# A cross-attention block: another order of the matmuls in the main loop, SyncE's queue ordered by hand, and another order of loads for the first two pairs

## The chip, the cores and the metric

The kernel runs on one core of a Trainium2 chip. A core has five engines that run side by side and wait for one another through semaphores: TensorE (PE, matmuls), VectorE (DVE), ScalarE (ACT), GpSimd (POOL) and SyncE (SP, which here only issues DMAs). ScalarE issues some DMAs too. The metric is the device time of one execution in microseconds, as the median of several runs. The profile shows one execution.

## What is computed

Inputs are `x` and `ctx_1024`, both 128 sequences of 128 tokens with 256 features, in float32. Every sequence goes through one block:

```python
q = (x @ Wq + bq), k = (ctx @ Wk + bk), v = (ctx @ Wv + bv)      # 16 heads of 16
scores = q k^T / sqrt(16);  scores = where(j < i, scores, -1e30)
attn = softmax(scores);  attn[:, :, 0, :] = 0
a = (attn v) @ Wo + bo
h = layer_norm(x + a, ln1_g, ln1_b)
out = layer_norm(h + relu(h @ W1 + b1) @ W2 + b2, ln2_g, ln2_b)   # W1: 256 x 1024
```

## The kernel before

**Tiles.** The 128 sequences are handled as 64 pairs `p` (256 tokens). Tokens of a pair are brought in twice: as blocks of 32 x 32 (`xb`, `cb`, `load`, line 80), which a VectorE block transpose turns into feature-major `xT` and `cT` (`tokens`, line 241), and as rows (`x`, `load_tokens`, line 97), which become the residual `xb` after `bov_r` is added (`add_bo`, line 248).

**One pair's way through the engines.** `queries`, `keys` and `values` (lines 265 to 311) are projections with full 128 x 128 matmuls; ScalarE copies their results out of PSUM into `qT`, `kT` and `vz`, and `values_out` issues a DMA that fills `vd` from ScalarE's queue. `scores(p, hi)` (line 315) makes the scores in small tiles of 32 rows x 64 columns: `hi` = 1 are queries 64 to 127 against 128 keys (16 matmuls of 256 columns), `hi` = 0 are queries 0 to 63 against 64 keys (16 matmuls of 128 columns); because of the mask the others are not needed. Softmax goes round three engines: VectorE adds the mask and takes the maximum (`mask`, `maximum`), GpSimd subtracts it, ScalarE takes the exponential (`exponential`), VectorE sums and inverts, GpSimd multiplies (`sums`). The upper scores are handled in two halves, `ONE` and `TWO`, the lower ones in one piece, `ALL`.

The weights must be transposed before they meet the values. `turn` (line 382) transposes 32 x 32 blocks on VectorE into `tb`, three instructions, and then moves the blocks between partitions by 16 DMAs `pT <- tb` on SyncE. For the first pairs and the last one `turn_on_pe` (line 406) does it on TensorE. `weigh` (line 424) multiplies `pT` with `vz` and `vd` in tiles of 128 x 32 into `pc`; `context` copies `pc` to `cxT`; `attention_out` makes `po`, `attention_sum` adds the residual and takes the statistics of the first norm, `norm1` applies it, and `turn_x1` brings the result into feature-major `x1T` by four DMAs to device memory and one back (`across`, line 230), all on SyncE.

The feed-forward part is `hidden` (`ph`, relu on ScalarE into `hT`) and `second` (`py`), 16 full matmuls each; `second_sum`, `stats`, `scale_and_shift`, `norm2`, `finish` and `store` make and store the second norm. `store` issues its DMA on ScalarE.

**The order.** `tc.manual_schedule` (line 60) says that TensorE, VectorE, ScalarE and GpSimd execute their instructions in the order in which the Python code calls them. SyncE is not in the list: a scheduler chooses the order of its DMAs. The loop at line 790 is software-pipelined. In step `p` it makes the scores and softmax of pair `p`, the context of pair `p - 1`, the projections of `p + 1`, the token transposes of `p + 2`, the hidden layer of `p - 2` and the second layer of `p - 3`. On TensorE a step of the main part reads: upper scores of `p`, `py` first half, lower scores of `p`, `py` second half, `pc`, `pq`, `po`, `pk`, `pv`, `ph`. Steps 2 to 5 have a `plan` of their own, in which the feed-forward part is filled in.

The first two pairs are written out (lines 712 to 779). `fold_norm1` computes, once, `W1`'s product with the first norm's shift (16 products of one column), `scale_w1` scales W1 by its gain, `fold_values` makes `bov_r`.

**Buffers.** `tb` and `pT` have one buffer each, `xT`, `cT`, `qT`, `kT`, `hT` two, and a bank of PSUM is one of four in turn (`bank`). Each DMA signals one of eight semaphores in turn, and a DMA waits until the one that used its semaphore before has landed, whichever queue issued it.

Of the kernel before, what the change touches and what calls it, by code (L numbers as in the profile page):

```python
# [13 lines left out]
P = 128  # L14
# [5 lines left out]
def tile_cross_attention_block(  # L20
# [26 lines left out]
    H = 16  # L47
# [9 lines left out]

    ET = mybir.EngineType
    ctx.enter_context(
        tc.manual_schedule(engines={ET.PE, ET.DVE, ET.Activation, ET.Pool})  # L60
    )

    const = ctx.enter_context(tc.tile_pool(name="const", bufs=1))
# [32 lines left out]

    def load_tokens(g, us=slice(0, 4)):
        if g not in tokens_of:
            tokens_of[g] = loads.tile([P, 4, D], F32, tag="x", name=f"x_{g}")
        nc.sync.dma_start(  # L100
            tokens_of[g][:, us], x[4 * g + us.start : 4 * g + us.stop].rearrange("b p d -> p b d")
        )


    def weight(w, name):
        n = w.shape[0] // P
        t = const.tile([P, n, w.shape[1]], F32, tag=name, name=name)
# [31 lines left out]
    table = const.tile([P, 2, 1], F32, tag="table", name="table")  # L139
    nc.scalar.activation(table, power, AF.Exp)  # L140

    b1_c = column(b1, "b1_c")
    w1 = weight(W1, "w1")
    load([1])
    wo = weight(Wo, "wo")
    bo_r = row(bo, "bo_r")
    load_tokens(0, slice(2, 4))
    g1_r = row(ln1_g, "g1_r")
    be1_r = row(ln1_b, "be1_r")
    bv_c = chunks(bv, "bv_c")  # L150
    g1_c = chunks(ln1_g, "g1_c")
    be1_c = chunks(ln1_b, "be1_c")
    load([2, 3])
    load_tokens(1)
    b2_r = row(b2, "b2_r")
    w2 = weight(W2, "w2")
    g2_r = row(ln2_g, "g2_r")
    be2_r = row(ln2_b, "be2_r")
    be1b_r = const.tile([P, D], F32, tag="be1b_r", name="be1b_r")
# [219 lines left out]

    def turn(p):


        st = states[p]
        tb = soft.tile([P, NS, (H + HH) * 32], F32, tag="tb", name=f"tb_{p}")
        at = 0
        for hi in (1, 0):
            sm = st["sm", hi].rearrange("p h j -> p (h j)")
            for t in range(sm.shape[1] // 1024):  # L390
                nc.vector.transpose(  # L391
                    tb[:, :, at : at + 256].rearrange("p j (n a) -> p n j a", a=32),
                    sm[:, t * 1024 : (t + 1) * 1024].rearrange(
                        "p (n j a) -> p n j a", j=NS, a=32
                    ),
                )
                at += 256
        pT = soft.tile([P, NS, (H + HH) * 32], F32, tag="pT", name=f"pT_{p}")
        for i in range(NS):
            for j in range(NS):  # L400
                nc.sync.dma_start(  # L401
                    pT[32 * j : 32 * j + 32, i, :], tb[32 * i : 32 * i + 32, j, :]
                )
        st["pT"] = pT.rearrange("p i (n a) -> p i n a", a=32)

    def turn_on_pe(p, hi, ts):

# [78 lines left out]
    def attention_sum(p):  # L486
        st = states[p]
        t1 = st["t1"] = ffn.tile([P, 2, D], F32, tag="t1", name=f"t1_{p}")
        nc.vector.tensor_tensor(
            t1, st.pop("po").rearrange("p (s d) -> p s d", s=2), st.pop("xb"), ALU.add  # L490
        )
        stats(p, t1, 1)
        deviation(p, 1)

    def norm1(p):
# [53 lines left out]

    b1e_c = const.tile([P, FC], F32, tag="b1e_c", name="b1e_c")  # L550

    def fold_norm1():

        ps = bank("ps_b1")
        for f in range(FC):
            for k in range(KC):
                nc.tensor.matmul(
                    ps[:, f : f + 1], w1[:, k, f * P : (f + 1) * P], be1_c[:, k : k + 1],
                    start=(k == 0), stop=(k == KC - 1),
                )  # L560
        nc.vector.tensor_tensor(b1e_c, ps[:, :FC], b1_c, ALU.add)

    def scale_w1():
        for k in range(KC):
# [33 lines left out]
        for k in range(KC):  # L598
            nc.scalar.copy(st["x1T"][:, :, :, k, :], pt[:, k])  # L599

    def hidden(p, fs):
        st = states[p]
        if fs[0] == 0:
            st["hT"] = ffn.tile([P, FC, TP], F32, tag="hT", name=f"hT_{p}")
        for f in fs[::2]:
            ph = bank(f"ph_{p}_{f}")
            for i in range(2):
                for k in range(KC):
                    nc.tensor.matmul(  # L609
                        ph[:, i * TP : (i + 1) * TP].rearrange("p (s i a) -> p s i a", s=2, a=32),  # L610
                        w1[:, k, (f + i) * P : (f + i + 1) * P], st["x1T"][:, :, :, k, :],
                        start=(k == 0), stop=(k == KC - 1),
                    )
            for i in range(2):
                nc.scalar.activation(  # L615
                    st["hT"][:, f + i, :], ph[:, i * TP : (i + 1) * TP], AF.Relu,
                    bias=b1e_c[:, f + i : f + i + 1], scale=1.0,
                )

    def second(p, s, fs=range(FC)):  # L620
        st = states[p]
# [102 lines left out]
    exponential(0, 1, ONE)  # L724
    values_out(0)
    maximum(0, 0, ALL)
    exponential(0, 1, TWO)
    queries(1)
    sums(0, 1, ONE)
    sums(0, 1, TWO)  # L730
    exponential(0, 0, ALL)
    keys(1)
    sums(0, 0, ALL)
    for which in "xc":
        tokens(2, which)
    values(1)
    values_out(1)
    fold_values()
    add_bo(0)
    load([4, 5])  # L740
    load_tokens(2)
    turn_on_pe(0, 1, range(2))
    scores(1, 1)
    mask(1, 1, 0)
    maximum(1, 1, ONE)
    turn_on_pe(0, 1, range(2, 4))
    turn_on_pe(0, 0, range(2))
    mask(1, 1, 1)
# [12 lines left out]
    queries(2)  # L761
    sums(1, 1, ONE)
    norm1(0)
# [11 lines left out]
    add_bo(1)  # L775
    add_bo(2)
    feed([("hidden", 0, 0)])
    turn_on_pe(1, 1, range(4))
# [7 lines left out]
        4: ([("hidden", 2, 0)], [("hidden", 2, 1)], [("second", 2, 0)]),  # L786
        5: ([("second", 2, 1)], [("hidden", 3, 0)], [("hidden", 3, 1)]),
    }
    waiting, late = [], []
    for p in range(2, NP):  # L790
        soon, end = p + 1 < NP, p == NP - 1
        first, then, finally_ = plan.get(
            p, ([("second", p - 3, 0)], [("second", p - 3, 1)], both("hidden", p - 2))
        )
        scores(p, 1)
        mask(p, 1, 0)
        maximum(p, 1, ONE)
        feed(first)
        mask(p, 1, 1)
        maximum(p, 1, TWO)  # L800
        scores(p, 0)
        mask(p, 0, 0)
        mask(p, 0, 1)
        exponential(p, 1, ONE)
        maximum(p, 0, ALL)
        exponential(p, 1, TWO)
        feed(then)
        sums(p, 1, ONE)
        sums(p, 1, TWO)
        summed = late + sum_up(first + then)  # L810
        exponential(p, 0, ALL)
        sums(p, 0, ALL)
        for q in waiting:
            finish(q)
        weigh(p - 1)
        context(p - 1)
        if soon:
            queries(p + 1)
        attention_out(p - 1)
        if not end:  # L820
            turn(p)
        attention_sum(p - 1)
        if soon:
# [44 lines left out]
    attention_out(p)  # L868
    second(p - 2, 1, range(FC // 2, FC))
    attention_sum(p)  # L870
    second_sum(p - 2)
    hidden(p - 1, range(FC))
    norm1(p)
# [72 lines left out]
```

## Time and profile before

| what | value |
| --- | --- |
| median of 3 runs | 1624.45 us (1621.69 to 1626.28) |
| the profiled execution | 1624.0 us, of it span 1622.2 us |
| busy TensorE / VectorE / GpSimd / ScalarE | 1602.6 / 1315.3 / 1274.9 / 765.6 us |
| granted clock of TensorE in the first three stretches of 40 us | 0.92, 0.95, 1.00 |
| DMAs `pT <- tb` | 976 on SyncE, 96 KB each, 2.1 us to landing |
| DMAs `out` and `vd` | 63 and 64 on ScalarE, 4.1 and 3.6 us to landing |
| mean busy share of the 16 DMA engines, per 40 us of the main part | about 0.6 |

Times are counted from the start of the span. A line of the timeline gives start, length, engine, line of the kernel, operation, what is written and read, the shapes, and the number of instructions merged; in brackets stands the idle time before it and what ended it. SPq and ACTq are the DMA-issuing sides of SyncE and ScalarE. A float32 matmul appears as two passes, so `pq`'s four matmuls are x8. The length of a matmul line includes the draining of the last pass, which overlaps the next line; from start to start is what it takes.

### The profile page before, as it was taken

How to read it: one execution, taken by the hardware profiler on the slowest of the kernel's cores; microseconds unless marked ns; L12 is line 12 of the kernel's file. 1: busy time of each engine (PE TensorE's matmuls, PEld its weight loads, DVE VectorE, ACT ScalarE, POOL GpSimd, SP SyncE). 2: the span in 40 equal slices, each digit the busy share in tenths (PEclk: the TensorE clock that was granted, in tenths of full speed). 3: DMA queues.
4: the chain of work that ended last, by engine and by line, in shares of the span. 5: the costliest groups of instructions: out<-in, count | busy, mean ns of one | idle time of the engine just before them, and what ended most of it. 6: DMA issues, size and time to landing. Idle time of an engine off the chain costs nothing.

```text
span 1622.2 us, 41250 instructions
## 1 busy us (share of the span) xinstructions
PE 1602.6 (99%) x16532; PEld 1338.3 (83%) x16532; DVE 1315.3 (81%) x1988; ACT 765.6 (47%) x1500; POOL 1274.9 (79%) x1105
## 2 busy tenths in 40 slices
PE   8999999999999999999999999999999999999998
PEld 6788888888888888888888888888888888888887
DVE  5789788888888888888888888888888888888852
ACT  4544444544444544444444445445444444445442
POOL 5788787887887887887887878878878878878882
PEclk9999999999999999999999999999999999999999
DMA  9345655656565665665565555566656656556430
GB/s 182 70 102 125 141 130 132 136 130 144 133 138 128 135 139 138 133 131 133 131 145 133 132 136 131 131 144 137 135 131 133 139 138 133 129 134 133 112 82 27
DMA packets 479998, 208.80 MB, mean 129 GB/s; under 512 B 352064, under 2 KB 448320, under 8 KB 479808
## 3 DMA queue, kind: packets, MB, share of 16 engines
q1 hardware_dynamic: 394864, 181.24, 50.2%
q10 hardware_dynamic: 84944, 24.92, 6.5%
q8 instruction: 132, 2.16, 0.6%
q14 instruction: 58, 0.48, 0.1%
HBM read 69.48 MB, written 32.24 MB: 63 GB/s over the span
## 4 chain that ended last, share of the span: by engine, by line
PE 94%; SPq 3%; DVE 1%; DMA 1%; issue 1%; POOL 0%; ACT 0%; POOLq 0%; ACTq 0%; DVEq 0%
PE py L625 27%; PE ph L609 26%; PE pq L259 7%; PE po L463 7%; PE pss L325 7%; PE pk L259 7%; PE pv L291 6%; PE pc L444 3%; PE pc L434 2%; SPq L401 1%; SPq L93 1%; PE py L637 1%; DVE sm L342 1%; DVE nmx L353 0%; PE ptp L417 0%
## 5 line engine op out<-in xcount | busy, mean ns | idle before, releaser
L354 POOL TENSOR_TENSOR sm<-sm,nmx 128x1024 f32<-128x1024 f32 x192 | 364.5, 1899 | 189.2 <-DVE nmx L353 185.8
L609 PE MATMUL ph<-x1T,w 128*128 128x256 f32 x2048 | 454.1, 379 | 2.1 <-ACT x1T L599 2.1
L625 PE MATMUL py<-w,hT 128*128 128x256 f32 x1952 | 453.6, 385 | 0.0
L609 PEld LDWEIGHTS ph<-x1T,w 128*128 128x128 f32 x2048 | 388.5, 190 | 56.8 <-ACT x1T L599 3.2
L625 PEld LDWEIGHTS py<-w,hT 128*128 128x128 f32 x1952 | 361.0, 190 | 76.9 <-ACT hT L615 21.9
L342 DVE TENSOR_TENSOR sm<-pss,neg 128x1024 f32<-128x1024 f32 (+1 forms) x256 | 237.7, 949 | 190.4 <-PE pss L325 190.4
L361 ACT ACTIVATE sm<-sm 128x1024 f32<-128x1024 f32 x192 | 203.0, 1058 | 342.5 <-POOL sm L354 342.4
L375 POOL TENSOR_TENSOR sm<-sm,rs 128x1024 f32<-128x1024 f32 x192 | 359.4, 1901 | 2.8 <-DVE rs L374 2.8
L615 ACT ACTIVATE hT<-ph,b1e_c 128x256 f32<-128x256 f32 x512 | 214.4, 471 | 184.7 <-PE ph L609 149.9
L391 DVE STREAM_TRANSPOSE tb<-sm 128x1024 f32<-128x1024 f32 x183 | 220.4, 1230 | 33.1 <-POOL sm L375 23.8
L353 DVE TENSOR_REDUCE nmx<-sm 128x8 f32<-128x1024 f32 (+1 forms) x192 | 234.2, 1220 | 6.6
L373 DVE TENSOR_REDUCE su<-sm 128x8 f32<-128x1024 f32 (+1 forms) x192 | 229.5, 1195 | 1.1 <-ACT sm L361 0.8
L281 ACT ACTIVATE kT<-pk,bkh,half 128x256 f32<-128x256 f32 x256 | 123.8, 565 | 160.4 <-PE pk L259 160.4
L325 PE MATMUL pss<-kT,qT 32*64 32x256 f32 (+1 forms) x4096 | 127.7, 334 | 5.7 <-DVE sm L342 3.4
L259 PE MATMUL pq<-xT,wq 128*128 128x256 f32 x512 | 129.6, 397 | 0.0
L463 PE MATMUL po<-wo,cxT 128*128 128x256 f32 x512 | 122.9, 384 | 1.4 <-ACT cxT L456 1.4
L509 POOL TENSOR_TENSOR x1b<-x,g_r 128x512 f32<-128x512 f32 x64 | 81.5, 1274 | 53.6 <-DVE x L501 53.6
L291 PE MATMUL pv<-wv,cT 128*128 128x256 f32 x512 | 121.0, 379 | 0.0
L259 PE MATMUL pk<-cT,wk 128*128 128x256 f32 x512 | 121.0, 379 | 0.0
L325 PEld LDWEIGHTS pss<-kT,qT 32*64 32x64 f32 x4096 | 76.5, 131 | 53.6 <-issue 41.8
L463 PEld LDWEIGHTS po<-wo,cxT 128*128 128x128 f32 x512 | 98.2, 192 | 15.4 <-ACT cxT L456 1.6
L259 PEld LDWEIGHTS pk<-cT,wk 128*128 128x128 f32 x512 | 97.4, 190 | 13.3
(86 smaller groups left out, 1687.6 us busy)
## 6 DMA issues: line engine op xcount, KB each, us to landing
pT<-tb SPq DMA_DIRECT2D x976, 96.0 KB, 2.1
out_dram<-t ACTq DMA_DIRECT2D x63, 256.0 KB, 4.1
xb<-in_x_dram SPq DMA_DIRECT2D x124, 128.0 KB, 4.4
cb<-in_ctx_dram SPq DMA_DIRECT2D x124, 128.0 KB, 4.4
x<-in_x_dram SPq DMA_DIRECT2D x31, 512.0 KB, 4.3
x1t<-tbx SPq DMA_DIRECT2D x236, 64.0 KB, 1.8
x1T<-x1t SPq DMA_DIRECT2D x59, 256.0 KB, 3.1
vd<-vz ACTq DMA_DIRECT2D x64, 128.0 KB, 3.6
```

What stands on the lines that cost most here:

```text
L259: nc.tensor.matmul(ps[:, m * TP : (m + 1) * TP], w[:, k, m * P : (m + 1) * P], src[:, k, :], start=(k == 0), stop=(k == KC - 1),)
L291: nc.tensor.matmul(pv[:, s * D : (s + 1) * D], st["cT"][:, k, s * P : (s + 1) * P], wv[:, k, :], start=(k == 0), stop=(k == KC - 1),)
L325: nc.tensor.matmul(sps[r // 2][s * HP : (s + 1) * HP, r % 2, m * 2 * n : (m + 1) * 2 * n].rearrange("p (e j) -> p e j", e=2), st["qT"][str ...
L342: nc.vector.tensor_tensor(st["sm", hi][:, part, :].rearrange("p (r n) j -> p r n j", r=2), st["sps", hi][t][:, :, : 4 * n].rearrange("p r ...
L353: nc.vector.tensor_reduce(nmx[:, part], sm[:, part, :], AX.X, ALU.max, negate=True)
L354: nc.gpsimd.tensor_tensor(sm[:, part, :], sm[:, part, :], nmx[:, part, None].to_broadcast([P, part.stop - part.start, n]), ALU.add,)
L373: nc.vector.tensor_reduce(su, sm[:, part, :], AX.X, ALU.add)
L375: nc.gpsimd.tensor_tensor(sm[:, part, :], sm[:, part, :], rs[:, :, None].to_broadcast([P, part.stop - part.start, n]), ALU.mult,)
L391: nc.vector.transpose(tb[:, :, at : at + 256].rearrange("p j (n a) -> p n j a", a=32), sm[:, t * 1024 : (t + 1) * 1024].rearrange("p (n j ...
L463: nc.tensor.matmul(po[:, s * D : (s + 1) * D], cxT[:, k, s, :], wo[:, k, :], start=(k == 0), stop=(k == KC - 1),)
L609: nc.tensor.matmul(ph[:, i * TP : (i + 1) * TP].rearrange("p (s i a) -> p s i a", s=2, a=32), w1[:, k, (f + i) * P : (f + i + 1) * P], st[ ...
L625: nc.tensor.matmul(st["py"][:, s * D : (s + 1) * D], st["hT"][:, f, s * P : (s + 1) * P], w2[:, f, :], start=(f == 0), stop=(f == FC - 1),)
```

## The change

**SyncE by hand.** SyncE joins the list of engines that keep the order of the code. The loads for later pairs are issued at the head of a step (`load_ahead`), the row tokens together with the context blocks, and the token buffer has two parts instead of three.

**A new step for pairs 7 to 62** (`steady`). On TensorE it reads: upper scores of `p`, both halves of `py`, `pc`, lower scores of `p`, `pq`, `po`, `pk`, `pv`, `ph`. VectorE, ScalarE and GpSimd follow that order: the context transpose of `p + 2` stands behind the upper maxima, the upper weights are transposed before the lower sums, the lower ones after the statistics and the token transpose. `turn` is split into `turn` (one block transpose) and `bring` (DMAs); eight of the 16 DMAs `pT <- tb` stay on SyncE, and eight go to ScalarE's queue between the relus of `hidden`: two behind the chunk pair 2, two behind 4, four behind 6. Pairs 2 to 6 and 63 keep the old step, with all 16 on SyncE.

**The first two pairs.** The loads of W1 come later, blocks of pairs 2 and 3 earlier; the token transposes of pair 1 and 2 are spread out; `fold_norm1` moves behind the lower scores of pair 1, and its sum with `b1` becomes `add_b1` behind the maxima.

```diff
-        tc.manual_schedule(engines={ET.PE, ET.DVE, ET.Activation, ET.Pool})
+        tc.manual_schedule(engines={ET.PE, ET.DVE, ET.Activation, ET.Pool, ET.SP})
...
-            tokens_of[g] = loads.tile([P, 4, D], F32, tag="x", name=f"x_{g}")
+            tokens_of[g] = loads.tile([P, 4, D], F32, tag="x", name=f"x_{g}", bufs=2)
...
-    b1_c = column(b1, "b1_c")
-    w1 = weight(W1, "w1")
     load([1])
     wo = weight(Wo, "wo")
     bo_r = row(bo, "bo_r")
+    bv_c = chunks(bv, "bv_c")
+    b1_c = column(b1, "b1_c")
+    g1_c = chunks(ln1_g, "g1_c")
+    be1_c = chunks(ln1_b, "be1_c")
+    load([2, 3], "x")
+    w1 = weight(W1, "w1")
+    load([2, 3], "c")
     load_tokens(0, slice(2, 4))
...
-    load([2, 3])
-    load_tokens(1)
     b2_r = row(b2, "b2_r")
     w2 = weight(W2, "w2")
+    load_tokens(1)
...
+    def bring(p, queue, which):
...
+        for u in which:
+            i, j = u // NS, u % NS
+            queue.dma_start(
+                st["pT whole"][32 * j : 32 * j + 32, i, :], st["tb"][32 * i : 32 * i + 32, j, :]
+            )
...
-    for which in "xc":
-        tokens(1, which)
     mask(0, 1, 1)
     maximum(0, 1, TWO)
-    fold_norm1()
     scores(0, 0)
+    tokens(1, "x")
+    exponential(0, 1, ONE)
+    values_out(0)
+    queries(1)
+    sums(0, 1, ONE)
     mask(0, 0, 0)
     mask(0, 0, 1)
+    tokens(1, "c")
...
     maximum(1, 1, TWO)
+    tokens(2, "x")
     weigh(0)
     context(0)
     scores(1, 0)
-    scale_w1()
+    fold_norm1()
...
     attention_out(0)
     exponential(1, 1, TWO)
+    scale_w1()
+    tokens(2, "c")
+    add_b1()
     attention_sum(0)
+    attention_stats(0)
...
+    def load_ahead(p):
+        if p % 2 == 0 and p + 4 < NP:
+            load([p + 4, p + 5], "x")
+        if p % 2 == 1 and p + 3 < NP:
+            load([p + 3, p + 4], "c")
+            load_tokens((p + 3) // 2)
+
+    def steady(p):
+        nonlocal waiting, late
+        scores(p, 1)
+        mask(p, 1, 0)
+        maximum(p, 1, ONE)
+        second(p - 3, 0)
+        mask(p, 1, 1)
+        maximum(p, 1, TWO)
+        exponential(p, 1, ONE)
+        second(p - 3, 1)
+        if p + 2 < NP:
+            tokens(p + 2, "c")
+        sums(p, 1, ONE)
+        exponential(p, 1, TWO)
+        summed = late + sum_up(both("second", p - 3))
+        sums(p, 1, TWO)
+        weigh(p - 1)
+        context(p - 1)
+        scores(p, 0)
+        queries(p + 1)
+        mask(p, 0, 0)
+        mask(p, 0, 1)
+        maximum(p, 0, ALL)
+        exponential(p, 0, ALL)
+        turn(p, 1, 0)
+        turn(p, 1, 1)
+        for q in waiting:
+            finish(q)
+        attention_out(p - 1)
+        attention_sum(p - 1)
+        sums(p, 0, ALL)
+        attention_stats(p - 1)
+        if p + 2 < NP:
+            tokens(p + 2, "x")
+        turn(p, 0, 0)
+        bring(p, nc.sync, range(NS * NS // 2))
+        keys(p + 1)
+        norm1(p - 1)
+        turn_x1(p - 1)
+        values(p + 1)
+        values_out(p + 1)
+        for q in waiting:
+            store(q)
+        add_bo(p + 1)
+        residual1(p - 1)
...
+        def share(f):
+            nonlocal at
+            n = 0 if f == 0 else NS if f == FC - 2 else NS // 2
+            bring(p, nc.scalar, range(at, at + n))
+            at += n
+
+        hidden(p - 2, range(FC), share)
+        late = []
+        for q in summed:
+            norm2(q)
+        waiting = summed
...
+        load_ahead(p)
+        if p > 6 and not end:
+            steady(p)
+            continue
         scores(p, 1)
...
-        if p % 2 == 0 and p + 4 < NP:
-            load([p + 4, p + 5], "x")
-            load_tokens(p // 2 + 2)
-        if p % 2 == 1 and p + 3 < NP:
-            load([p + 3, p + 4], "c")
```

More of the change, by code (lines that the diff above doesn't have):

```diff
@@ L149, in tile_cross_attention_block @@
     be1_r = row(ln1_b, "be1_r")
-    bv_c = chunks(bv, "bv_c")
-    g1_c = chunks(ln1_g, "g1_c")
-    be1_c = chunks(ln1_b, "be1_c")
-    load([2, 3])
-    load_tokens(1)
     b2_r = row(b2, "b2_r")
     w2 = weight(W2, "w2")
+    load_tokens(1)
     g2_r = row(ln2_g, "g2_r")
@@ L378, in sums, with turn @@
         )
-    def turn(p):
+    def turn(p, hi, t):
         st = states[p]
[L386 to L404, printed above, removed]
+        if "tb" not in st:
+            st["tb"] = soft.tile([P, NS, (H + HH) * 32], F32, tag="tb", name=f"tb_{p}")
+        at = (t if hi else 2) * 256
+        nc.vector.transpose(
+            st["tb"][:, :, at : at + 256].rearrange("p j (n a) -> p n j a", a=32),
+            st["sm", hi].rearrange("p h j -> p (h j)")[:, t * 1024 : (t + 1) * 1024].rearrange(
+                "p (n j a) -> p n j a", j=NS, a=32
+            ),
+        )
+    def bring(p, queue, which):
+        st = states[p]
+        if "pT" not in st:
+            pT = st["pT whole"] = soft.tile([P, NS, (H + HH) * 32], F32, tag="pT", name=f"pT_{p}")
+            st["pT"] = pT.rearrange("p i (n a) -> p i n a", a=32)
+        for u in which:
+            i, j = u // NS, u % NS
+            queue.dma_start(
+                st["pT whole"][32 * j : 32 * j + 32, i, :], st["tb"][32 * i : 32 * i + 32, j, :]
+            )
     def turn_on_pe(p, hi, ts):
@@ L491, in attention_sum, with attention_stats @@
         )
-        stats(p, t1, 1)
+    def attention_stats(p):
+        stats(p, states[p]["t1"], 1)
         deviation(p, 1)
@@ L550, in tile_cross_attention_block @@
     b1e_c = const.tile([P, FC], F32, tag="b1e_c", name="b1e_c")
+    ps_b1 = None
     def fold_norm1():
-        ps = bank("ps_b1")
+        nonlocal ps_b1
+        ps = ps_b1 = bank("ps_b1")
         for f in range(FC):
@@ L560, in fold_norm1, with add_b1 @@
                 )
-        nc.vector.tensor_tensor(b1e_c, ps[:, :FC], b1_c, ALU.add)
+    def add_b1():
+        nc.vector.tensor_tensor(b1e_c, ps_b1[:, :FC], b1_c, ALU.add)
     def scale_w1():
@@ L599, in turn_x1_on_pe, with hidden @@
             nc.scalar.copy(st["x1T"][:, :, :, k, :], pt[:, k])
-    def hidden(p, fs):
+    def hidden(p, fs, between=None):
         st = states[p]
@@ L618, in hidden @@
                 )
+            if between:
+                between(f)
     def second(p, s, fs=range(FC)):
@@ L715, in tile_cross_attention_block @@
     values(0)
-    for which in "xc":
-        tokens(1, which)
     mask(0, 1, 1)
     maximum(0, 1, TWO)
-    fold_norm1()
     scores(0, 0)
+    tokens(1, "x")
[3 more added lines that the diff above has]
+    sums(0, 1, ONE)
     mask(0, 0, 0)
     mask(0, 0, 1)
-    exponential(0, 1, ONE)
-    values_out(0)
+    tokens(1, "c")
+    exponential(0, 1, TWO)
     maximum(0, 0, ALL)
-    exponential(0, 1, TWO)
-    queries(1)
-    sums(0, 1, ONE)
+    keys(1)
     sums(0, 1, TWO)
+    values(1)
     exponential(0, 0, ALL)
-    keys(1)
+    turn_on_pe(0, 1, range(2))
+    values_out(1)
     sums(0, 0, ALL)
[L734 to L742, printed above, removed]
     scores(1, 1)
@@ L745, in tile_cross_attention_block @@
     maximum(1, 1, ONE)
+    fold_values()
     turn_on_pe(0, 1, range(2, 4))
     turn_on_pe(0, 0, range(2))
+    add_bo(0)
     mask(1, 1, 1)
     maximum(1, 1, TWO)
+    tokens(2, "x")
     weigh(0)
@@ L775, in tile_cross_attention_block @@
     add_bo(1)
+    load([4, 5])
+    load_tokens(2)
     add_bo(2)
@@ L788, in tile_cross_attention_block @@
     }
+    def load_ahead(p):
[50 more added lines that the diff above has]
+        for q in summed:
+            stats(q, states[q]["t2"], 2)
+        for q in summed:
+            scale_and_shift(q)
+        at = NS * NS // 2
+        def share(f):
[5 more added lines that the diff above has]
+        late = []
+        for q in summed:
+            norm2(q)
+        waiting = summed
     waiting, late = [], []
@@ L820, in tile_cross_attention_block @@
         if not end:
-            turn(p)
+            turn(p, 1, 0)
+            turn(p, 1, 1)
+            turn(p, 0, 0)
+            bring(p, nc.sync, range(NS * NS))
         attention_sum(p - 1)
+        attention_stats(p - 1)
         if soon:
@@ L870, in tile_cross_attention_block @@
     attention_sum(p)
+    attention_stats(p)
     second_sum(p - 2)
```

## The prediction

> **What bounds the kernel now.** I read the page from the top: busy shares, then the chain that ended last.
>
> ```profile
> span 1622.2 us, 41250 instructions
> ...
> PE 1602.6 (99%) x16532; PEld 1338.3 (83%) x16532; DVE 1315.3 (81%) x1988; ACT 765.6 (47%) x1500; POOL 1274.9 (79%) x1105
> ...
> PE 94%; SPq 3%; DVE 1%; DMA 1%; issue 1%; POOL 0%; ACT 0%; POOLq 0%; ACTq 0%; DVEq 0%
> ```
>
> TensorE is busy 99% of the span and is 94% of the chain. A busy TensorE need not be one at its peak, so I went on to the timeline of TensorE over one step of the main loop (start, length, what).
>
> ```profile
> 1004.34 7.07 PE L609 MATMUL ph<-x1T,w 128*128 128x256 f32 x32
> 1011.34 1.12 PE L325 MATMUL pss<-kT,qT 32*64 32x256 f32 x32
> 1012.39 3.72 PE L625 MATMUL py<-w,hT 128*128 128x256 f32 x16
> 1016.04 0.84 PE L325 MATMUL pss<-kT,qT 32*64 32x128 f32 x32
> 1016.81 3.72 PE L625 MATMUL py<-w,hT 128*128 128x256 f32 x16
> 1020.46 0.43 PE L434 MATMUL pc<-pT,vd 128*32 128x64 f32 x16
> ...
> 1021.94 1.99 PE L259 MATMUL pq<-xT,wq 128*128 128x256 f32 x8
> 1023.77 1.89 PE L463 MATMUL po<-wo,cxT 128*128 128x256 f32 x8
> ```
>
> There is no gap, and no wait inside the step; the same pattern returns every 24.61 us (the chain's ph starts at 217.03, 241.63, 266.24). So only TensorE's own work can shorten a step. The next matmul group starts 1.73 us after po, eight passes of 0.216 us. By that rate the 32 passes of ph need 6.90 us and took 7.00; each 16 of py need 3.45 and took 3.65; the 8 of pq need 1.73 and took 1.83. What is over belongs to the borders between full 128*128 matmuls and the small tiles (32*64 of pss, 128*32 of pc): about 0.093 us when full matmuls end and 0.104 us when they begin again. A step has three such round trips, 3 x 0.197 = 0.59 us.
>
> **The change, part by part.**
>
> *The new step, pairs 7 to 62, 56 steps.* The matmuls are the same, in another order: the two halves of py stand together, and the lower scores (pss 32x128) come after pc, small tile after small tile. By the rows: ph 7.00 + pss 1.05 + py 32 x 0.2158 + 0.197 = 7.10 + pc 1.48 + pss 0.77 + pq 1.83 + po 1.73 + pk 1.72 + pv 1.73 = 24.41 us. That is one round trip less, 0.197 us, and 56 x 0.197 = 11.0 us.
>
> Against this stands a rule of the Trainium skill (TensorEngine Tiling (Array Packing), Key Properties): changing the tiling mode, not only the tile, drains TensorE. The row first: every group of small tiles already ends in about 0.09 us without a new pass (pc's 1.48 us includes it). By the rule the border pc to pss, 128*32 to 32*64, is a mode change too. If it costs only the drain that is inside pc's 1.48, the saving is 0.197; if it costs another 0.1, as entering pss from ph does, it is 0.10, 5.5 us in all; if two small modes needed no drain it is 0.29, 16 us. No run has this border unmixed with a wait. I take 0.197, nearest to the rows.
>
> *Whether the other engines keep up.* I laid the new order out by hand from the durations of the rows, with time zero at the first score matmul of a step. Upper scores: mask 1.14, maximum 2.41, mask 3.54, maximum 4.81 to 6.02; GpSimd subtracts 3.70 to 5.60 and 6.10 to 8.00; ScalarE's exponentials end at 6.69 and 9.09; VectorE's sums end at 7.96 and 10.36 with the context transpose (6.02) and the second sum (8.28) between. pc runs from 8.15, the lower scores from 9.63 to 10.4; mask 10.56, maximum to 13.07, subtraction to 15.05, exponential to 16.14, sum to 17.41, product (after the two of finish) 17.81 to 19.71, last transpose into tb to 21.00. VectorE ends at 23.5 and is next needed at 25.55; GpSimd ends near 26.0 and is needed at 28.1. Both have some 2 us left. py needs its last two hT chunks at about 28; they are written by about 26.
>
> *The eight DMAs moved to ScalarE's queue.* This is the price.
>
> ```profile
> 1005.32 0.60 ACTq L305 DMA_DIRECT2D vd<-vz  x1
> 1006.03 0.69 ACTq L545 DMA_DIRECT2D out_dram<-t  x1
> ...
> 1017.02 1.06 ACT L361 ACTIVATE sm<-sm 128x1024 f32<-128x1024 f32 x1 [2.88 <-POOL sm L354]
> ```
>
> ```profile
> L401 SPq DMA_DIRECT2D pT<-tb x16: 507/590/801, 1004.1 to 1016.4; - x16
> ```
>
> ScalarE does nothing else while it issues: the copy behind vd starts only as that issue ends. A pT issue took SyncE 0.51 to 0.80 us, median 0.59; vd, also SBUF to SBUF, took ScalarE 0.60 while SyncE was issuing pT beside it. I take D = 0.59 with 0.04 between two, eight times: 5 us a step for an engine that is busy 12. They stand after the second, third and fourth relu pair, and behind them wait relu, norm2 and then the next step's first exponential, for which VectorE's sum waits. This closes a ring: exponential 1.12, sum, reciprocal and the sum of py 1.99, sum and reciprocal 1.41, two masks 1.30, maximum 1.29, subtraction 1.93, exponential 0.96, four kT 1.86, two vz 0.72, vd issue and copy 0.95, out issue 0.74, four relu pairs 2.96, norm2 with its waits 1.2, eight spacings 0.35: 18.8 us + 8 D. At D = 0.59 that is 23.5, under 24.41 by 0.9. The cover is gone at D = 0.70, and from there each 0.1 us of D costs 0.8 us a step.
>
> The skill's rule here (DMA: Bandwidth & Descriptors, Issuing engines are not separate DMA queues) is that both queues run on the same 16 DMA engines, so a second queue saves issue time only. By the rule the 16 transfers get no faster; by the rows, SyncE's 16 in 12.86 us become eight of 0.63 = 5 us there and eight here, all issued by about 4.0 in the next step. With 2.1 us to landing the last is there at 6, and pc starts at 8.15. Even a landing twice as slow, 4.2 us, comes in time.
>
> Each DMA also waits for an earlier one on its semaphore. ScalarE's third follows out, issued at 19.6 and landing 4.1 us later, 23.7, just before it is due at 23.9: nothing, or 0.5 us if out lands late.
>
> *SyncE's row by hand.* Loads at the head of a step, then eight pT, four x1t, one x1T: about 4 + 5 + 2 + 0.4 us and a wait of 2 for x1t, under 24. x1T lands at 33.5 and ph needs it at 41.8. Loads issued by 10 land by 15; their first reader comes a step later. The token buffer has two parts instead of three; its reader, the sum with bov, ran a step earlier. Cost nothing; SyncE's slack is the cover. Pairs 2 to 6 keep their step: zero, within 1 us either way.
>
> *The first two pairs.*
>
> ```profile
> 14.71 3.63 PE L557 MATMUL ps_b<-be_c,w 128*128 128x1 f32 x32
> ...
> 39.62 3.78 PE L463 MATMUL po<-wo,cxT 128*128 128x256 f32 x8
> ```
>
> ```profile
> 17.72 0.71 DVE L244 STREAM_TRANSPOSE cT<-cb 128x512 f32<-128x512 f32 x1 [1.60 <-DMA cb<-in_ctx_dram]
> ...
> 32.46 0.71 DVE L244 STREAM_TRANSPOSE cT<-cb 128x512 f32<-128x512 f32 x1 [3.22 <-DMA cb<-in_ctx_dram]
> ```
>
> VectorE loses 1.60 + 3.22 us waiting for context blocks, and starts the mask of pair 1 at 33.46. Reordered, that mask follows the last sum of pair 0, near 28.2; the lower scores of pair 1 end near 34.3 instead of 39.6. But the 3.63 us of the sum over b1, which lay under VectorE's work, now stand in TensorE's row ahead of po, and nothing covers them: po starts near 37.9 instead of 39.62, 1.7 us gained. po ran at half clock here (3.78 us for eight passes, 1.89 later; the granted clock is 0.92 and 0.95 over the first two stretches of 40 us, then 1.00). If TensorE is granted full clock there, 3 us more; if the b1 sum or the keys run at half clock, 3 us less. I take 1.5, from a gain of 4.5 to a loss of 2.
>
> **Sum**, against the profiled execution's 1624.0 us (span 1622.2 + 1.8; the median of the runs is 1624.45): 1624.0 - 11.0 - 1.5 = 1611.5 us.
>
> **Rivals.**
> - *The border costs a full round trip.* Then nothing is saved in the step; the mode rule speaks for it, the drain already inside pc's 1.48 us against it. Only the start remains: 1622.5 us. That is also the case in which the change does not do what it says.
> - *ScalarE's ring becomes the bound* (the other side). Place: the pT issues between relu pairs; decisive from D = 0.70, slower than before from 0.725. For it: the slowest pT issues took 0.80 us, beside an out issue, and SyncE now issues pT at the same moment. Against: vd beside pT is not slowed. At 0.80 a step is 18.8 + 6.4 = 25.2 us, 56 x 0.6 = 33.6 us more, less 1.5: 1656 us; at 0.74, 24.72 and 1629.
> - *pT lands after pc is due.* 2.1 us of slack; the 16 DMA engines were busy only about 60% in these steps. At 3 us late by crowding, 0.9 x 56 = 50 us lost: 1662 us. Unlikely.
> - *The border is free and the start runs at full clock*: 1624.0 - 16 - 4.5 = 1603.5 us.
>
> **How the numbers follow.** Forecast 0.60 (1606 to 1617), free border 0.14, no saving 0.09, ring 0.14, late pT 0.03. Under 0.3%, 4.9 us, this kernel's runs (1621.69 to 1626.28) can't be told from no change. Faster: the first two, and 0.03 of the third: 0.77; same 0.07; slower 0.16. The range reaches from the free border to a ring at D just under 0.75: 1603 to 1632, leaving a tenth above and less below.
>
> **What would show it.** Right: ph starts 24.41 us apart; the lower pss directly behind pc; no wait of TensorE on DMA or ScalarE in the loop; pT issues on ScalarE under 0.70 us; the first upper exponential still released by GpSimd; scores of pair 2 near 54.8 instead of 56.28. Wrong: steps over 24.61, with VectorE's sums waiting for the exponential or pc for pT; pT issues of 0.75 us and more.

## The result

The changed kernel took 1606.4 us (median of 4 runs, 1604.26 to 1607.59) against 1625.37 us for the kernel before (4 runs, measured beside it). The ratio is 0.9885, with a 95% interval of 0.9865 to 0.9906: 1.15% or some 18.7 us faster. The forecast was 1611.5; the time lies at the lower end of its main case, 1606 to 1617.

The page of the changed kernel, with the lines that answer to those shown of before:

```profile
span 1602.5 us, 41277 instructions
...
PE 1581.9 (99%) x16532; PEld 1333.4 (83%) x16532; DVE 1368.0 (85%) x1988; ACT 758.9 (47%) x1500; POOL 1281.9 (80%) x1105
...
PE 94%; DVE 3%; POOL 1%; ACT 1%; issue 1%; DMA 1%; ACTq 0%; SPq 0%; POOLq 0%; DVEq 0%
```

TensorE is still busy 99% of the span and still 94% of the chain: it does the same 16532 passes, in 20.7 us less. The timeline of TensorE over one step (start, length, what):

```profile
998.42 1.12 PE L326 MATMUL pss<-kT,qT 32*64 32x256 f32 x32
999.47 7.17 PE L636 MATMUL py<-w,hT 128*128 128x256 f32 x32
1006.57 0.43 PE L436 MATMUL pc<-pT,vd 128*32 128x64 f32 x16
...
1008.05 0.69 PE L326 MATMUL pss<-kT,qT 32*64 32x128 f32 x32
1008.67 1.99 PE L260 MATMUL pq<-xT,wq 128*128 128x256 f32 x8
...
1015.68 7.07 PE L618 MATMUL ph<-x1T,w 128*128 128x256 f32 x32
1022.68 1.12 PE L326 MATMUL pss<-kT,qT 32*64 32x256 f32 x32
```

The upper scores return after 1022.68 - 998.42 = 24.26 us, where the kernel before needed 24.61 and the forecast said 24.41. From start to start, py takes 7.10, pc 1.48, pq 1.83 and ph 7.00, as forecast. The lower scores behind pc take 1008.67 - 1008.05 = 0.62 us instead of the 0.77 that was carried over from the old place.

Where the 19.7 us between the two spans come from, by the starts of the upper scores of pairs 2, 7 and 63:

| part | before | after | gained |
| --- | --- | --- | --- |
| start to pair 2 | 56.28 | 55.47 | 0.81 |
| pairs 2 to 6 | 118.37 | 117.97 | 0.40 |
| pairs 7 to 62 | 1378.09 | 1359.65 | 18.43 |
| pair 63 and the end | 69.46 | 69.44 | 0.02 |

The third row is 56 x 0.345 = 19.3 us, less 0.8 in one step of 25.07, in which py waited for hT, and 0.07 in the last.

### The profile page after: what moved, and what is told of

Same layout as the page of the kernel before. It is cut to its first block, busy times and chain, and to the rows that moved or that the text cites. A ratio compares the mean times of both kernels' runs of the same rounds, so it can differ in the third digit from the quotient of the medians.

```text
span 1602.5 us, 41277 instructions
## 1 busy us (share of the span) xinstructions
PE 1581.9 (99%) x16532; PEld 1333.4 (83%) x16532; DVE 1368.0 (85%) x1988; ACT 758.9 (47%) x1500; POOL 1281.9 (80%) x1105
## 4 chain that ended last, share of the span: by engine, by line
PE 94%; DVE 3%; POOL 1%; ACT 1%; issue 1%; DMA 1%; ACTq 0%; SPq 0%; POOLq 0%; DVEq 0%
PE ph L618 27%; PE py L636 26%; PE pq L260 7%; PE po L465 7%; PE pk L260 7%; PE pv L292 6%; PE pss L326 6%; PE pc L446 3%; PE pc L436 2%; DVE sm L343 1%; DVE nmx L354 1%; PE py L648 1%; PE ptp L419 0%; POOL sm L376 0%; ACT kT L282 0%
## 5 line engine op out<-in xcount | busy, mean ns | idle before, releaser
L636 PE MATMUL py<-w,hT 128*128 128x256 f32 x1952 | 438.9, 382 | 0.5 <-ACT hT L624 0.5
L636 PEld LDWEIGHTS py<-w,hT 128*128 128x128 f32 x1952 | 365.6, 190 | 71.1 <-issue 15.5
L376 POOL TENSOR_TENSOR sm<-sm,rs 128x1024 f32<-128x1024 f32 x192 | 364.0, 1898 | 71.7 <-DVE rs L375 68.8
L374 DVE TENSOR_REDUCE su<-sm 128x8 f32<-128x1024 f32 (+1 forms) x192 | 233.5, 1216 | 51.1 <-ACT sm L362 47.7
L389 DVE STREAM_TRANSPOSE tb<-sm 128x1024 f32<-128x1024 f32 x183 | 219.8, 1227 | 28.3 <-POOL sm L376 27.7
L534 ACT ACTIVATE t<-t,nb,sd 128x256 f32<-128x256 f32 x124 | 67.7, 593 | 181.8 <-DMA pT<-tb 110.7
L326 PE MATMUL pss<-kT,qT 32*64 32x256 f32 (+1 forms) x4096 | 118.1, 334 | 3.0 <-DVE sm L343 1.7
L271 ACT ACTIVATE qT<-pq,bqs_c 128x256 f32<-128x256 f32 x128 | 53.6, 470 | 122.4 <-PE pq L260 122.4
```

The costliest lines, as they stand in the source:

```text
L326: nc.tensor.matmul(sps[r // 2][s * HP : (s + 1) * HP, r % 2, m * 2 * n : (m + 1) * 2 * n].rearrange("p (e j) -> p e j", e=2), st["qT"][str ...
L374: nc.vector.tensor_reduce(su, sm[:, part, :], AX.X, ALU.add)
L376: nc.gpsimd.tensor_tensor(sm[:, part, :], sm[:, part, :], rs[:, :, None].to_broadcast([P, part.stop - part.start, n]), ALU.mult,)
L389: nc.vector.transpose(st["tb"][:, :, at : at + 256].rearrange("p j (n a) -> p n j a", a=32), st["sm", hi].rearrange("p h j -> p (h j)")[:, ...
L636: nc.tensor.matmul(st["py"][:, s * D : (s + 1) * D], st["hT"][:, f, s * P : (s + 1) * P], w2[:, f, :], start=(f == 0), stop=(f == FC - 1),)
```

## The experiments

Ten kernels were run, each beside the kernel before on the same chip. "Step" is the distance between the upper scores of successive pairs in the profiled execution; the times of TensorE's groups are from start to start.

| kernel | step, us | median, us | ratio to before (95%) |
| --- | --- | --- | --- |
| e1_old_step | 24.61 | 1623.95 | 1.0006 (0.9996 to 1.0017) |
| e2_lower_between | 24.61 | 1622.67 | 1.0002 (0.9991 to 1.0013) |
| e3_lower_inside_pc | 24.40 | 1614.07 | 0.9946 (0.9933 to 0.9958) |
| e4_lower_in_halves | 24.80 | 1632.6 | 1.0063 (1.0047 to 1.0079) |
| e5_lower_before_pc | 24.26, later 24.33 | 1610.52 | 0.9923 (0.9894 to 0.9951) |
| e6_all_on_sync | 25.1 | 1650.56 | 1.0169 (1.0135 to 1.0204) |
| e7_twelve_on_act | 29.4 | 1867.65 | 1.1507 (1.1407 to 1.1607) |
| e8_masks_first | 24.46 | 1615.15 | 0.9961 (0.9946 to 0.9976) |
| e9_joined | 24.72 | 1644.51 | 1.0149 (1.0120 to 1.0178) |
| e10_joined_again | 24.07 to 24.24 | 1629.08 | 1.0047 (1.0030 to 1.0065) |

### Is it the step, or the start and SyncE's order?

```diff
-        if p > 6 and not end:
-            steady(p)
-            continue
```

> The new start and SyncE's hand order are kept, all pairs keep the old step (upper scores, half of py, lower scores, half of py, pc, with 16 pT transfers on SyncE). Theory (the gain sits in the new step): the step stays 24.61 us, pair 2 starts 0.8 us and pair 7 1.2 us earlier than before, so about 1.2 us gained in all, ratio 0.999, time near 1624. Rival (SyncE's order or the start carries the gain): 1615 or less.

The step is 24.61 us, and the time can't be told from before: the interval allows a gain of at most 0.65 us (0.04%). The start and SyncE's order by hand carry nothing that can be measured; all of the gain is in the new step.

### Is it the place of the lower scores?

```diff
         second(p - 3, 0)
...
+        scores(p, 0)
         second(p - 3, 1)
...
         context(p - 1)
-        scores(p, 0)
         queries(p + 1)
```

> The new step with one thing undone: the lower scores stand again between the two halves of py; the split of the pT issues and the order of the other engines stay. Theory (TensorE's borders): the step goes back to 24.61 us, 0.35 more than 24.26, and the time to about 1606.4 + 56 x 0.35 = 1626. Rival (the other engines or the queues carry the gain): the step stays 24.26, 1606.

The step is 24.61 us again and the whole gain is gone, though everything else of the new step stayed: the eight transfers on ScalarE, the divided block transposes, the order of VectorE and GpSimd. So it is TensorE's own row. But 0.345 us a step is more than the 0.197 that the rows of before give for a round trip between full and small tiles.

### What does a border cost?

Two kernels add a border and no matmul. In the first the lower scores stand inside pc, in the second half of them stand between the halves of py:

```diff
...
-        weigh(p - 1)
+        weigh(p - 1, [0])
+        scores(p, 0)
+        weigh(p - 1, [1])
         context(p - 1)
-        scores(p, 0)
```

> The lower scores stand between the two halves of pc, so that a step has two borders between small groups of different tiles (128*32 to 32*64 and back) where the changed kernel has one. Theory (a border between small tiles is free): the step stays 24.26 us, time 1606. Rival (a change of the tile's mode drains TensorE, 0.10 us each): 24.36, 1612. Rival (a full round trip): 24.46 to 24.6, 1617 to 1625.

```diff
...
+        scores(p, 0, [0])
         second(p - 3, 1)
...
-        scores(p, 0)
+        scores(p, 0, [1])
```

> Half of the lower scores' passes go between the two halves of py, half stay behind pc: no pass more, one round trip between full and small tiles more, and the border between pc and the scores stays. If such a round trip costs what the change saved, 0.345 us: step 24.61, time 1626. If it costs 0.197, as the rows of before gave it, and the rest of the saving belongs to the scores standing behind pc: 24.46, time 1617.

The first has a step of 24.40, 0.14 more than the changed kernel. TensorE's timeline over the four groups:

```profile
1012.42 0.55 PE L437 MATMUL pc<-pT,vd 128*32 128x64 f32 x16
...
1013.34 0.69 PE L326 MATMUL pss<-kT,qT 32*64 32x128 f32 x32
1013.96 0.43 PE L437 MATMUL pc<-pT,vd 128*32 128x64 f32 x16
...
1014.77 1.99 PE L260 MATMUL pq<-xT,wq 128*128 128x256 f32 x8
```

The lower scores take 0.62 here too. The two halves of pc take 0.81 us each in the median of 49 steps, 1.62 together, where the undivided pc takes 1.48 (in the step shown the first half takes 0.92, which the median does not have). A group of small tiles therefore carries a fixed 0.14 us of its own, and it doesn't matter whether full or small matmuls stand before it. The 0.14 lies between the second forecast, 0.10, and the third, 0.20 and more: the border is neither free nor a round trip.

The second has a step of 24.80, 0.535 more than the changed kernel and above both expectations. Its two halves of the scores take 0.55 us between the halves of py and 0.40 behind pc: the same 16 passes, 0.15 apart. So 0.15 us belongs to the place between the halves of py, beside the 0.20 of the round trip and a fixed part of some 0.19 for a group of scores more.

> The two small groups change places: the lower scores come directly ahead of pc instead of directly behind it. If a border between small groups costs the same in both directions, the step stays 24.26 us, time 1606. If what the runs so far add up to holds (0.15 us more for score passes that follow full matmuls than for score passes that follow pc, and 0.20 for the interruption of py): 7.10 + 0.77 + 1.48 and the rest, step 24.41, time 1615.

```diff
+        scores(p, 0)
         weigh(p - 1)
         context(p - 1)
-        scores(p, 0)
```

This one says that the 0.15 us are no border at all. Directly behind the full matmuls of py the lower scores take 0.62 us, not the expected 0.77, and the step is 24.26 at first. (Later steps have 24.33 and some over 25: pc then takes 1.54, the 0.07 us more lying ahead of its ninth pass and those behind it, and py waits for hT. Why the other engines keep up less well in this order was not followed.)

### The 0.15 us: a wait that no list of waits showed

What does the place between the halves of py have that the place behind it has not? The timelines of TensorE and VectorE of the kernel before, around the lower scores:

```profile
1014.93 1.21 DVE L342 TENSOR_TENSOR sm<-pss,neg 128x1024 f32<-128x1024 f32 x1
...
1016.04 0.84 PE L325 MATMUL pss<-kT,qT 32*64 32x128 f32 x32
```

The lower scores write the PSUM banks of the upper ones, which VectorE's second mask reads until 1014.93 + 1.21 = 1016.14. TensorE comes to them at 1016.04, has free banks for its first two passes, and starts the third at 1016.197, right after the mask. The line is 0.84 long against 0.69 in the changed kernel. No list of waits has it, because the engine never stands idle: the two passes begun at 1016.04 are on record as running until 1016.36, past the start of the third. To test it, the lower scores go back between the halves of py, and VectorE masks both halves before its first maximum:

```diff
         mask(p, 1, 0)
+        mask(p, 1, 1)
         maximum(p, 1, ONE)
         second(p - 3, 0)
-        mask(p, 1, 1)
         maximum(p, 1, TWO)
         exponential(p, 1, ONE)
+        scores(p, 0)
         second(p - 3, 1)
...
         context(p - 1)
-        scores(p, 0)
```

> The lower scores stand between the two halves of py, as in the kernel before, but VectorE masks both halves of the upper scores before it takes their first maximum, so that the second mask ends 1.2 us earlier and the banks that the lower scores write are free when TensorE comes to them. Theory (0.15 us of the old step was TensorE waiting inside the lower scores for that mask): the lower scores take 0.62 instead of 0.77 us there too, the step is 24.61 - 0.15 = 24.46, the time near 1616. Rival (0.15 is the price of changing from full to small tiles): 0.77 and 24.61, 1623.

```profile
1005.57 2.36 DVE L343 TENSOR_TENSOR sm<-pss,neg 128x1024 f32<-128x1024 f32 x2
...
1009.25 0.69 PE L326 MATMUL pss<-kT,qT 32*64 32x128 f32 x32
1009.87 3.72 PE L636 MATMUL py<-w,hT 128*128 128x256 f32 x16
```

Both masks end at 1007.9, 1.3 us before the lower scores start. They take 0.62 us, the step is 24.46, and the time 1615.15 us. This divides the gain: 24.61 - 24.46 = 0.15 us was TensorE waiting for VectorE inside a group, and 24.46 - 24.26 = 0.20 us is the round trip between full and small tiles.

### The transfers: was the split needed, and how near is ScalarE's ring?

> The new step with all 16 pT transfers on SyncE, none on ScalarE. Theory (the issue time on one queue is too long, so the split is needed): the last of the 16 is issued 21.0 + 16 x 0.63 = 31.1 us after the step's begin and lands 2.8 later, at 33.9, where pc is due at 24.26 + 8.15 = 32.4; TensorE waits for pT in each step, the step is 25.2 to 25.8 us, time 1660 to 1690. Rival (the split is not needed): step 24.26, time 1606.

```diff
-        bring(p, nc.sync, range(NS * NS // 2))
+        bring(p, nc.sync, range(NS * NS))
...
-        hidden(p - 2, range(FC), share)
+        hidden(p - 2, range(FC))
```

TensorE's waits, in total, times and longest:

```profile
PE pc L436 <- DMA x1t<-tbx: 15.3, 18, 1.9
PE pc L436 <- DMA pT<-tb: 12.9, 14, 1.7
```

The step is 25.1 us and the time 1650.56, both just below the expected. (The view puts 18 of the waits to x1t, which pc does not read; its transfers use the same eight semaphores.) With the landing of 2.2 us that this run shows instead of the 2.8 assumed, the last transfer is there at 31.1 + 2.2 = 33.3 and pc is due at 32.4: 0.9 late, which is what a step has more. The split is a condition of the new order, since pc would otherwise wait for pT.

> The new step with twelve of the 16 pT transfers on ScalarE and four on SyncE. Theory of ScalarE's ring, 18.8 us + n x D with D = 0.54 to 0.60 us as the changed kernel has it: 25.3 to 26.0 us a step, VectorE's sums waiting for the exponential, TensorE waiting behind them; time 1665 to 1705. Rival (ScalarE has room, the ring is not near): step 24.26, time 1606.

```diff
-        bring(p, nc.sync, range(NS * NS // 2))
+        bring(p, nc.sync, range(NS))
...
-            n = 0 if f == 0 else NS if f == FC - 2 else NS // 2
+            n = 0 if f == 0 else NS
```

ScalarE's, TensorE's and VectorE's waits:

```profile
ACT hT L624 <- DMA pT<-tb: 259.7, 98, 4.3
ACT t L534 <- DMA pT<-tb: 175.3, 40, 5.5
```

```profile
PE pc L436 <- DMA pT<-tb: 99.8, 34, 4.1
PE pc L436 <- issue: 50.2, 18, 3.9
```

```profile
DVE su L374 <- ACT sm L362: 237.5, 114, 5.6
```

The cause is ScalarE's queue, as expected; the size is not, and the place of TensorE's wait only in part. The step is 29.4 us, not 25.3 to 26.0. VectorE's sums do wait for the exponential, but TensorE waits above all at pc: 99.8 us for pT and 50.2 for which the view names no engine, over half of the 5.1 us by which each of some 55 steps is longer, and only 20.7 for hT. So pT is late here, beside the ring that was expected. An issue still takes 0.60 us, and 18.8 + 12 x 0.60 = 26.0. On top of that comes ScalarE standing at an issue until an earlier transfer has landed whose semaphore the new one uses: in the step at 1020 us it stood 0.81, 0.51 and 2.07 us, together 3.4. More transfers on ScalarE meet each other's landings. That 26.0 + 3.4 is just 29.4 is luck, because the same sum is too long in the changed kernel, as the next lines show. The granted clock was lower as well, 0.94 from 300 to 1500 us against 1.00 in the changed kernel. How the 29.4 divides between late pT, the ring and the clock stays open.

In the changed kernel the same waits are there, smaller, and TensorE doesn't see them:

```profile
1021.65 0.47 ACT L624 ACTIVATE hT<-ph,b1e_c 128x256 f32<-128x256 f32 x1
1023.72 0.52 ACTq L404 DMA_DIRECT2D pT<-tb  x1
1024.28 0.84 ACT L624 ACTIVATE hT<-ph,b1e_c 128x256 f32<-128x256 f32 x2 [2.17 <-PE pss L326]
```

ScalarE is free at 1022.12 and issues at 1023.72: 1.6 us of waiting. In the median a step has 2.1 us of it, at the fourth, sixth and eighth issue. The sum 18.8 + 8 x 0.60 + 2.1 = 25.7 is more than the step, 24.26, so the sum is too long by at least 1.4 us. The rows show one reason:

```profile
1018.94 1.57 ACT L624 ACTIVATE hT<-ph,b1e_c 128x256 f32<-128x256 f32 x4 [0.35 <-POOL sm L376]
1020.04 1.19 ACTq L404 DMA_DIRECT2D pT<-tb  x2
```

The first issue starts at 1020.04, while the relus ahead of it run until 1020.51. In the median 1.9 us of a step's pT issues lie beside ScalarE's work in this way, and the sum counted everything one behind the other: 25.7 - 1.9 = 23.8, under the step.

### One interruption less

If an interruption of the full matmuls costs 0.20 us, the next one to take away is that of the upper scores. From pair 8 on they are made one step ahead, behind pc:

```diff
+    def joined(p):
...
+        second(p - 3, 0)
+        second(p - 3, 1)
+        scores(p, 0)
+        weigh(p - 1)
+        scores(p + 1, 1)
...
```

> A version made on the findings: from pair 8 on the upper scores of the next pair stand directly behind pc too, so that a step has one interruption of the full matmuls where the changed kernel has two; queries and keys are computed one pair further ahead, tb has two buffers, and the first transfers are not waited for. If an interruption costs 0.197 us wherever it is: step 24.06, 55 steps, time near 1596, 0.6% under the changed kernel. If only the wait on the mask mattered: 24.26, 1606. If the upper scores now wait for the two masks of the lower ones behind pc: 24.3 and more, 1608 or more.

It is slower. VectorE is late with the masks: the upper scores take 1.64 us in the median instead of 1.05, waiting for banks. (TensorE also stops nine times, 10.8 us in all, in a way that the next kernel shows.) In the timelines the first norm stands out (VectorE, two instructions), here and in the next kernel:

```profile
1020.38 3.26 DVE L505 TENSOR_SCALAR x<-t,mv,sd 128x256 f32<-128x256 f32 x2 [0.80 <-POOL sd L486]
```

```profile
1014.68 0.74 DVE L505 TENSOR_SCALAR x<-t,mv,sd 128x256 f32<-128x256 f32 x2
```

> The joined version again, with what made VectorE late in e9_joined taken out: the first part of GpSimd's row is the subtraction that the exponential waits for (finish and the second norm's scales come later), the first norm of VectorE stands where GpSimd has nothing to run, the token transposes fill VectorE's wait for the deviation, ph stands ahead of the keys and values so that ScalarE has room for its eight transfers, t2 has three buffers. If VectorE now masks in time, an interruption less per step shows: 24.06 to 24.12 us, 1597 to 1603. If VectorE's own work (some 23 us a step) stays the limit: 24.3 to 24.7, 1610 to 1645, and the changed kernel is the better one.

With VectorE's and GpSimd's order mended (and ph ahead of the keys and values, so that ScalarE issues earlier), the upper scores wait no more, and most steps are 24.07 to 24.24 us: the 0.20 is there a second time. But the kernel is slower than the changed one, 1629.08 us. About 7.6 us are lost once at the end, where a po waits for cxT. And in two places, from step 21 and from step 44, four steps in a row take 25.4 to 28.3 us. There TensorE stops, eight times in all, in the second half of the upper scores or just behind them, without any semaphore:

```profile
562.47 1.08 PE L326 MATMUL pss<-kT,qT 32*64 32x256 f32 x9 [1.90 <-issue]
```

Counted in all instructions of TensorE's queue (matmuls, weight loads and the semaphore instructions between them), the four stops of the first place are exactly 512 apart, those of the second as well, and the two places are 12,032 = 47 x 256 apart. The nine stops of e9 fit the same grid to one instruction. In the queue table of the page instructions are moved in blocks of 16 KB:

```profile
q8 instruction: 132, 2.16, 0.6%
```

132 blocks are what TensorE's 33,755 instructions make at 256 to a block. And each of the 17 stops of the two kernels ends 1.3 to 1.9 us after such a block has landed; the stop that ends at 562.47 does so behind a block moved from 559.95 to 561.14. So TensorE stood waiting for its next block of instructions, in steps in which the 320 matmuls and loads of small tiles pass in 3.1 us. (The changed kernel has 256 in 2.1 us there; its one wait without a releaser, 0.5 us at pc, does not lie on the grid.) Behind the stop at 562.47 the granted clock was 0.5 for 3.4 us, and pq took 3.06 us instead of 1.83. A seam of blocks in the small tiles is not enough, though: from 611 to 1072 us seams fall there without a stop. Why the block comes late in some steps only stays open.

Mending the end would bring this version to about 1621 us, not below 1606, so it was left there; the changed kernel is the fastest of all that were run.

## Why the prediction was right, and where it was off

- **"So only TensorE's own work can shorten a step."** Right for more than half of the gain: with the lower scores put back (e2) the step is the old one, and the chain is TensorE before and after. But e8 differs from e2 in VectorE's order alone, and its step is 0.15 us shorter; that is the next point.
- **"There is no gap, and no wait inside the step."** This is the step of the working that failed. The kernel before had 0.15 us of wait inside its lower scores, in every step. The list of waits doesn't name it, since passes still under way covered it; the length of the line did (0.84 for passes that need 0.69). The forecast took 0.77 us for the lower scores from that row and carried it to the new place, where they take 0.62. That is 56 x 0.15 = 8.4 us that the sum missed, on the good side by luck: the new place was chosen for its neighbours, not for the banks that are free there.
- **One round trip less, 0.197 us.** Right in mechanism and size: 0.20 by e8 against the changed kernel.
- **The mode rule** (the Trainium skill, TensorEngine Tiling (Array Packing), Key Properties). The value taken, a drain that is already inside pc's 1.48 us, is what the runs show: pc takes 1.48 before pq and before the scores, and the scores take 0.62 behind pc and behind py. The drain of a change between two small modes is not free, though: each group of small tiles carries 0.14 to 0.19 us (e3, e4), whatever stands before it.
- **ScalarE's transfers.** D was put at 0.59; the trace of the changed kernel has

```profile
L404 SPq DMA_DIRECT2D pT<-tb x528: 507/591/1909, 74.3 to 1534.4; - x176
L404 ACTq DMA_DIRECT2D pT<-tb x448: 513/538/2019, 194.6 to 1537.0; - x150
```

  that is 0.54 us in the median and 0.60 in the mean for ScalarE, under the 0.70 at which it decides. Two readings around it were off, and it is luck that they nearly cancel. The wait of an issue for an earlier landing, "nothing, or 0.5 us", is 2.1 us a step. And "ScalarE does nothing else while it issues" is too strong: 1.9 us of the issues of a step lie beside the instructions ahead of them, and already in the kernel before the issue of out began at 1006.03 while the copy ahead of it ran, from 1005.96 for 0.37 us. ScalarE's row did become tight. The sign that was named, the first upper exponential released by GpSimd, held in 17 of the 56 steps, against all 56 before; in the others it stood directly behind ScalarE's own work. VectorE's sums waited 47.7 us for exponentials in all, against 0.8. In steps of 24.26 TensorE never saw it.
- **pT lands late.** It lands after 2.8 to 2.9 us instead of 2.1, within the factor of two that was allowed for. TensorE waited 0.3 us for it, once.
- **SyncE's order by hand, pairs 2 to 6.** Put at nothing: 0.4 us gained in pairs 2 to 6 of the profiled execution. The ten other kernels, which keep these pairs as they are, need 117.1 to 118.6 us for them, against 118.37 before, so this is not told from nothing.
- **The first two pairs, 1.5 us.** The profiled execution shows 0.81, those of e1 to e6, e8 and e9 1.1 to 2.8; in e7 and e10 pair 0 already starts 2 us later and pair 2 is 3.3 and 3.5 us behind the kernel before; the medians of e1 show nothing. The forecast had the parts right: no context transpose waits now, and pair 1's lower scores end at 34.08. What differs between executions is when TensorE goes to half clock. In the changed kernel it came early and the sum over b1 ran into it, in e1 later:

```profile
34.08 4.89 PE L564 MATMUL ps_b<-be_c,w 128*128 128x1 f32 x32
38.83 3.76 PE L465 MATMUL po<-wo,cxT 128*128 128x256 f32 x8
```

```profile
33.88 3.73 PE L564 MATMUL ps_b<-be_c,w 128*128 128x1 f32 x32
37.47 2.59 PE L465 MATMUL po<-wo,cxT 128*128 128x256 f32 x8
```

  The granted clock between 36 and 38 us was 0.60 in the changed kernel and 1.00 in e1; between 40 and 42 us it was 0.50 in both. Apart from e7 and e10, the traces with this start fall into two groups. Six (e1, e2, e3, e5, e6, e9) have 3.4 us of half clock from 18.0 to 18.9 us on and 3.4 more from 38.5 to 39.4 on, and reach pair 2 between 2.1 and 2.8 us earlier than the kernel before. Three (the changed kernel, e4, e8) have none near 18 us but 6.8 us of it from 36.2 to 36.4 on, and gain 0.8 to 1.2. What sends an execution into one group or the other was not tried.
- **The rivals.** The border at full price (1622.5) and the late pT fell. The ring fell as a bound of the changed kernel; with four transfers more on ScalarE (e7) its queue is the bound, by late pT at least as much as by the ring. The free border (1603.5) fell in its reason, though its time is as near as the forecast's: 0.29 us of its step were to come from borders, where 0.20 did, and 0.15 came from a wait.

By the measured parts the sum is 1624.0 - 56 x 0.345 + 0.8 (the one late step) - 0.8 (start) - 0.4 = 1604.3 us, the profiled execution's own time (its span and 1.8).

## What to carry to other kernels

Compare the length of a group with that of the same group elsewhere, or with passes times the price of a pass, before its time is called work: a wait that is covered by passes still under way is in no list of waits, and here it was nearly half of the gain. Putting groups of small tiles side by side saves one round trip, 0.20 us here, each time, but the groups keep their own 0.14 to 0.19 us, so a group that is only divided costs. Before transfers are moved to a busy engine's queue, count what an issue waits for as well as what it takes: 0.6 us of issue brought another 0.3 of waiting each at eight transfers, though part of it lay beside the engine's own work, and twelve made the kernel 15% slower.

## What was not expected of the hardware

- TensorE can run out of instructions: with some 320 matmuls and weight loads in 3.1 us it stopped for 0.5 to 2.4 us at seams 512 instructions apart, until 1.3 to 1.9 us after a block of instructions had landed (e9, e10). The Trainium skill (Runtime: NRT & Kernel Launch, Instruction fetch mechanics) gives the blocks of 16 KiB and 256 instructions that fit these distances, and says that the fetch is mostly hidden; here it was not.
- The first norm's two VectorE instructions took 0.42 us each in the kernel before, 0.80 in the changed one, 1.49 in e9 and 0.43 in e10, in the mean. Sorted by what GpSimd is at as they begin, one takes 0.36 to 0.42 us with no GpSimd instruction under way, 1.28 to 1.36 beside the sum that makes xb (1.3 us long), and 1.97 to 2.00 beside a product of 1.9 us; e9 has 56 of the last, e10 one. That fits the exclusive lock of VectorE and GpSimd on a shared port pair (the Trainium skill, SBUF — State Buffer, SBUF: two separate sides). No run changed this alone.
